# A two-layer CIN kernel: the hand-over between the layers, the place of one product in every stage, and the order of the last sums

## The chip, the core and the metric

The kernel runs on one core of a Trainium2 chip. The metric is the device time of one execution in microseconds (us). Times inside an execution are given in us from the start of the profiled span. The engines are named as the profile names them: PE (matmuls; PEld is its weight load), DVE (vector), ACT (scalar), POOL (GpSimd) and SP (issues transfers).

## The reference

Two "compressed interaction" layers work on x of 4096 rows, 32 fields and 16 embedding positions, which is 65,536 sites (row times position) of 32 values. A layer multiplies each of its channels with each field, multiplies the products with a weight matrix and normalises each output channel over all sites:

```
def _cin_layer(out, x, W, b, gamma, beta):
    h = einsum('rne,rfe->rnfe', out, x).reshape(r, -1, e)
    h = einsum('rce,oc->roe', h, W) + b[None, :, None]
    return _batchnorm(h, gamma, beta)        # over rows and positions
h1 = _cin_layer(x, x, W1, ...)               # 1024 products -> 128 channels
out, direct1 = h1[:, :64], h1[:, 64:]
direct2 = _cin_layer(out, x, W2, ...)        # 2048 products -> 128 channels
y = concatenate([direct1, direct2], axis=1).sum(axis=-1)
```

So half of layer 1 feeds layer 2, and the batch norm of layer 1 must be known before layer 2 can start: this is the boundary of the layers.

## The kernel before

**Layer 1** (lines 261 to 521) goes through 128 tiles of 512 sites. For each, DVE multiplies two loaded operands (L370), PE multiplies with W1 (L402), ACT copies the 128 result rows out of the accumulator bank (a PSUM bank, `ps`), and the 64 kept rows go to memory, to be read back in layer 2. The last four tiles (`ENDING = 4`) are handled apart: their kept halves come first, so that the statistics close early; then, still in layer 1's program, PE makes the other halves (L431), which only the direct output needs, and ACT copies these out of their banks into `ed` (the function `evict`, L515). Between the two, the scale and shift of the kept channels are computed, spread over the partitions by a tiny matmul (`keep_ps`) and copied by DVE to `keep` (L507). In the order of ACT's queue the two evictions of tile pair c = 62 come first (`queue("act", evict)`), then the first factor of layer 2; the two evictions of c = 63 are put on the list `sums_left` (it is the list `late_evictions`), from which each stage of layer 2 takes one.

**Layer 2** (L813 to L885) is one matrix product done by a fast scheme of the Strassen kind. Sites are cut into two halves and taken 512 at a time from each, so c runs from 0 to 63; the contraction is cut into four groups of fields and channels, the *stages* k = 0 to 3 of each c. I write (c,k) for a stage. In each stage:

- ACT makes two factors, `f1` and `f2` (`factor`, L647): kept rows scaled and shifted by `keep`, written to one of two PSUM buffers. It needs `keep`. It also copies a block `b11` of the products there.
- DVE makes products `zz` in two instructions (`multiply`, L637): the first, with `f1`, gives the blocks B11 and B21; the second, with `f2`, gives T3 and B22. Each block has two slices q = 0, 1 of 512 sites. The very first stage (0,0) does it in four smaller instructions, by q (`multiply_part`, L645).
- The sum T2 has two slices: POOL makes `t2[0]` (`sum_first`, L676), DVE makes `t2[1]` (L635). From these POOL makes T1 and T4 in one instruction over 2048 elements (`sum_rest`, L685; the tile is `t14`). Only at the last stage (63,3) this is in two parts, T1 and then T4.
- PE multiplies with 64 columns of weights. A product has two matmuls (q = 0, 1), and a matmul two passes in the trace; two products that write different 64-row halves run side by side, as a pair. `x2` makes X2 from B21, `x31` makes X3 (B22) and X1 (B11), `x67` makes X6 (T2) and X7 (T3), and `x54` makes X5 (T1) and X4 (T4). `x54` of a stage is not run in its own stage but in the next: the loop calls `waiting.x54()` first (L863), then `x2`, `x31` and `x67` of its own. So the products that need POOL's long instruction have a stage's time to wait for it. Stage (0,0) uses eight ordinary products and no T sums (`ordinary`).

The sums of one c lie in four banks, `x21`, `x62`, `x34` and `x57`; the pool has six banks, so c + 1 reuses those of c, and first those of layer 1. When c is done, a generator `combine` (L745) puts the seven sums together into four output blocks in `e`. Its steps are placed between the instructions of the next c's stages on ACT and DVE:

- ACT copies X1 (twice, with biases, into `both`) and X2 from `x21`.
- DVE adds `x62` to `both`; ACT makes `u2`; DVE adds `x57` to get `u3`.
- ACT copies half of `u3` into `e[low, 0]`; DVE adds `x34` to `u3`, giving `e[:, 1]` (L773: the blocks C12 and C21), and adds `x57` to `e[:, 0]` (L780: C22).
- Then the statistics: for most c, ACT sums squares about a centre (`add_square`, L569, two per c) into a column of `squares`; the centre itself comes at c = 0 from two `bn_stats` and `bn_aggr` of DVE (`first`, `moments`). The last two c use `bn_stats` of DVE (L795).
- DVE reduces `e` over the 16 positions (L800).

The **last stage** (63,3) is `at_last` (L727): after `waiting.x54()` of (63,2) it makes X6 and X1, then X2, then X5 and X7, then X3 and X4. Its `combine` has no further stage to hide under; it is followed by the closing statistics, scale and shift (L135 to L156), the scaling of the outputs (L899, L907) and their transfers.

Each engine works through its own list in order. `queue` (L226) fixes that the instructions of an engine stay in the order in which the program makes them, so the order of calls in the loop is the order of execution.

Of the kernel before, what the change touches and what calls it, by code (L numbers as in the profile page):

```python
# [43 lines left out]
ALU = mybir.AluOpType  # L44
AX = mybir.AxisListType

P = 128
# [3 lines left out]
T = 512  # L51
NC = HALF // T
# [8 lines left out]
STAGES = (3, 0, 1, 2)  # L61
# [7 lines left out]
def tile_cin(ctx: ExitStack, tc: tile.TileContext, xa, xb, xr, w1, w1m, w2, bn, out):  # L69
# [156 lines left out]
    def queue(engine, make):  # L226

        with tc.issue_after(lasts[engine].ins) if engine in lasts else nullcontext():
            lasts[engine] = make()
        return lasts[engine]  # L230
# [30 lines left out]
    with ExitStack() as one:  # L261
# [56 lines left out]

        pss = {}
        eds = {}  # L320
        late_evictions = []
        kept = {}

        def finish(t):
# [174 lines left out]
        for c in range(NC - ENDING // 2, NC):  # L499
            eds[c] = epool.tile([P, T], FP, tag="ed", name="ed")  # L500
            ks = tuple(2 * c + half - ending for half in range(2))
            if c < NC - 1:

                add_halves(banks, zs, 1, ks, False, False)
                add_leftovers_halves(banks, zr, 1, ks)
                matmul(keep_ps, spread, blocks, True, True)
                queue("dve", lambda: nc.vector.tensor_copy(keep, keep_ps))  # L507
            else:
                add_halves(banks, zs, 1, ks, True, True)
            for half, k in enumerate(ks):  # L510
                at = half_of[1 - half]
                bias = (b1, b1_swapped)[half][at]
                to = eds[c][half_of[half]]

                def evict(to=to, at=at, bias=bias, k=k):  # L515
                    return nc.scalar.activation(to, banks[k][at], AF.Identity, bias=bias)  # L516

                if c < NC - 1:
                    queue("act", evict)
                else:  # L520
                    late_evictions.append(evict)

    direct = const.tile([P, 2], FP, tag="direct", name="direct")

# [43 lines left out]
    def add_square(c, s, e):  # L568
        return nc.scalar.activation(  # L569
            unread, e[:, s], AF.Square, bias=center[:, s], accum_out=squares[:, s, c : c + 1]  # L570
        )
# [104 lines left out]
        queue("pool", lambda: nc.gpsimd.tensor_tensor(t2[:, 0], z[:, 1, 0], z[:, 0, 0], ALU.add))  # L676
        return t2

    def sum_rest(z, b11, t2, apart):

        t14 = upool.tile([P, 2, 2, T], FP, tag="t14", name="t14")
        add(t2[:, 1], z[:, 1, 1], b11)
        twice = t2.unsqueeze(1).to_broadcast([P, 2, 2, T])
        for k in (slice(0, 1), slice(1, 2)) if apart else (slice(0, 2),):
            queue("pool", lambda: nc.gpsimd.tensor_tensor(t14[:, k], z[:, 2:4][:, k], twice[:, k], ALU.subtract))  # L685
        return t2, t14

    class Stage:
# [7 lines left out]
                t2, t14 = t  # L696
                self.t2, self.t1, self.t4 = ([x[:, q] for q in range(2)] for x in (t2, t14[:, 0], t14[:, 1]))

        def one(self, x, k, b, q):
            self.sums.matmul(x, self.w[q][k], b[q], self.ends and q == 1)  # L700

        def ordinary(self):
            for q in range(2):
# [20 lines left out]
                self.one(6, 5, self.t2, q)  # L724
                self.one(7, 6, self.t3, q)

        def at_last(self):  # L727

            for q in range(2):
                self.one(6, 5, self.t2, q)  # L730
                self.one(1, 0, self.b11, q)
            self.x2()
            for q in range(2):
                self.one(5, 4, self.t1, q)
                self.one(7, 6, self.t3, q)
            for q in range(2):
                self.one(3, 7, self.b22, q)
                self.one(4, 3, self.t4, q)
# [6 lines left out]
    def combine(c, sums_):  # L745

        x21, x62, x34, x57 = sums_.banks
        both = cpool.tile([P, T], FP, tag="both", name="both")
        act(both[low], x21[high])
        act(both[high], x21[high], bias=b2_swapped[high])  # L750
        e = cpool.tile([P, 2, T], FP, tag="e", name="e")
        act(e[high, 0], x21[low])
        yield

        add(both, both, x62)
        if c == NC - 1:

            add(e[high, 0], e[high, 0], both[high])
        yield
        u2 = cpool.tile([P, T], FP, tag="u2", name="u2")  # L760
        act(u2[low], both[low], bias=b2[low])
        act(u2[high], both[low], bias=b2_swapped[low])
        yield

        u3 = cpool.tile([P, T], FP, tag="u3", name="u3")
        add(u3, u2, x57)
        yield
        act(e[low, 0], u3[high])
        if c < NC - 1:
            act(x57[high], both[high])  # L770
        yield

        add(e[:, 1], u3, x34)  # L773
        yield
        if 0 < c < MOST:
            queue("act", lambda: add_square(c, 1, e))
        yield

        rows = slice(0, P) if c < NC - 1 else low
        add(e[rows, 0], e[rows, 0], x57[rows])  # L780
        yield
        if c == 0:
            for s in range(2):
                dve(lambda: nc.vector.bn_stats(first[:, s], e[:, s]))
            dve(find_center)
            for s in range(2):
                act(center[:, s], moments[:, s, 0:1], scale=-1.0)
        if c < MOST:
            for s in range(2 if c == 0 else 1):
                queue("act", lambda: add_square(c, s, e))  # L790
        else:
            at = slice(1 + 2 * (c - MOST), 3 + 2 * (c - MOST))
            for s in range(2):
                stats = groups_of[s][:, at].rearrange("p a b -> p (a b)")
                dve(lambda: nc.vector.bn_stats(stats, e[:, s]))  # L795
                if s == 0:
                    queue("act", lambda: swap_group(at))
        yield
        dve(
            lambda: nc.vector.tensor_reduce(  # L800
                d2[:, :, c, :], e.rearrange("p s (r e) -> p s r e", e=EMB), AX.X, ALU.add
            )
        )
        if c % 16 == 15 or c == MOST - 1:
            sums_left.extend(lambda s=s: add_total(c // 16, s) for s in range(2))
        if c == MOST - 1:
            for s in range(2):
                sums_left.extend(most(s))
            sums_left.append(lambda: swap_group(slice(0, 1)))
        yield  # L810


    sums_left = late_evictions  # L813

    steps, steps_before = iter(()), iter(())
    waiting = None

    following = loaded(0)
    f1 = factor(following[0][STAGES[0]], STAGES[0], 0)
    for c in range(NC):  # L820
        raw, b, bx = following
        sums_ = Sums()

        for k, i in enumerate(STAGES):

            z = z2pool.tile([P, 4, 2, T], FP, tag="zz", name="zz")
            t = None
            if c == k == 0:

                f2 = factor(raw[i], i, 1)  # L830
                for q in range(2):
                    multiply_part(z[:, 0::3], f1, b, q)
                    multiply_part(z[:, 1:3], f2, bx, q)
            else:
                multiply(z[:, 0::3], f1, b)
                if k == 1:

                    next(steps, None)
                f2 = factor(raw[i], i, 1)
                b11 = factors.tile([P, T], FP, tag="f", name="b11")  # L840
                act(b11, z[:, 0, 1])
                if k == 1:

                    next(steps, None)
                multiply(z[:, 1:3], f2, bx)
                t2 = sum_first(z)

            next(steps_before if k == 0 else steps, None)
            if k == 3 and idle:
                dve(idle.pop(0))  # L850
            if c > 0 or k > 0:
                t = sum_rest(z, b11, t2, (c, k) == (NC - 1, 3))
            if k < 3:
                f1 = factor(raw[STAGES[k + 1]], STAGES[k + 1], 0)
            elif c + 1 < NC:
                following = loaded(c + 1)
                f1 = factor(following[0][STAGES[0]], STAGES[0], 0)

            next(steps, None)
            for _ in range(min(len(sums_left), 4 if c == NC - 1 else 1)):  # L860
                queue("act", sums_left.pop(0))
            stage = Stage(sums_, i, z, t, k == 3)
            if waiting:  # L863
                waiting.x54()
            if c == k == 0:
                stage.ordinary()
            elif (c, k) == (NC - 1, 3):
                stage.at_last()
            else:
                stage.x2()  # L870
                stage.x31()
                stage.x67()
            if c > 0 or k > 0:
                waiting = stage

            if c == 9 and k == 2:
                queue("act", direct_factors)
            if 10 <= c < 14 and k == 2:
                queue("act", lambda: scale_direct(c - 10))
            if c == 15 and k == 2:  # L880
                with tc.issue_after(loads[-1].ins):
                    write_direct()
        steps, steps_before = combine(c, sums_), steps
# [90 lines left out]
```

## Time and profile before

| what | value |
|---|---|
| median of 4 runs (lowest to highest) | 2049.69 us (2049.47 to 2050.06) |
| the profiled execution: its own time | 2050.06 us |
| its span, first to last instruction | 2048.3 us |
| PE busy | 2030.2 us, 99% |
| DVE busy | 1958.9 us |
| POOL busy | 1488.7 us, nearly all of it from 499 us on |
| ACT busy | 1186.1 us |
| layer 2's first matmul | 492.93 us |
| layer 2's last matmul begins | 2033.86 us |
| granted clock of PE | 0.998 |

The span is what the trace covers; the device time is 1.75 us longer. PE's busy share is close to the whole, but PE's matmuls overlap, so the way to see whether PE waits is the distance from one matmul to the next in the timeline, not the busy share. A "pair" in the timeline is two rows that start within some hundredths of a us, one for each half of the array; while PE is not held up, one pair of passes starts every 0.43 us.

### The profile page before, as it was taken

How to read it: one execution, taken by the hardware profiler on the slowest of the kernel's cores; microseconds unless marked ns; L12 is line 12 of the kernel's file. 1: busy time of each engine (PE TensorE's matmuls, PEld its weight loads, DVE VectorE, ACT ScalarE, POOL GpSimd, SP SyncE). 2: the span in 40 equal slices, each digit the busy share in tenths (PEclk: the TensorE clock that was granted, in tenths of full speed). 3: DMA queues.
4: the chain of work that ended last, by engine and by line, in shares of the span. 5: the costliest groups of instructions: out<-in, count | busy, mean ns of one | idle time of the engine just before them, and what ended most of it. 6: DMA issues, size and time to landing. Idle time of an engine off the chain costs nothing.

```text
span 2048.3 us, 24470 instructions
## 1 busy us (share of the span) xinstructions
PE 2030.2 (99%) x8506; PEld 719.3 (35%) x8506; DVE 1958.9 (96%) x1519; ACT 1186.1 (58%) x1912; POOL 1488.7 (73%) x518
## 2 busy tenths in 40 slices
PE   9999999999999999999999999999999999999997
PEld 3444444443333333333333333333333333333332
DVE  8998988988999999999999999999999999999997
ACT  4555555554556666565666555656656565566554
POOL 0000000002999999999999999999999999999996
PEclk9999999999999999999999999999999999999999
DMA  9999999996777776777776667777766777776661
GB/s 393 361 351 368 353 362 370 367 363 186 171 179 180 178 173 169 199 174 183 179 176 167 175 170 180 174 183 178 175 169 171 176 174 182 179 175 172 174 155 41
DMA packets 112092, 440.70 MB, mean 215 GB/s; under 512 B 13024, under 2 KB 13024, under 8 KB 103520
## 3 DMA queue, kind: packets, MB, share of 16 engines
q1 hardware_dynamic: 105552, 418.43, 73.0%
q10 hardware_dynamic: 6416, 20.72, 2.7%
q8 instruction: 66, 1.08, 0.2%
q14 instruction: 58, 0.48, 0.1%
HBM read 417.07 MB, written 22.02 MB: 214 GB/s over the span
## 4 chain that ended last, share of the span: by engine, by line
PE 97%; DVE 1%; POOL 1%; DMA 0%; ACT 0%; SPq 0%; issue 0%; DVEq 0%; POOLq 0%
PE x L671 74%; PE ps L402 21%; PE ps L363 2%; PE ps L431 1%; DMA b<-in_xb 0%; POOL t L685 0%; DVE zz L645 0%; DVE zz L640 0%; POOL t L676 0%; DVE z L370 0%; DVE d L899 0%; ACT u L632 0%; ACT ed L516 0%; DVE e L635 0%; ACT both L632 0%
## 5 line engine op out<-in xcount | busy, mean ns | idle before, releaser
L685 POOL TENSOR_TENSOR t<-zz,t 128x2048 f32<-128x2048 f32 (+1 forms) x256 | 1166.3, 4556 | 20.9 <-DVE t L635 1.1
L671 PE MATMUL x<-zz,s_sb 128*64 128x512 f32 x2048 | 922.5, 592 | 0.7 <-PE ps L431 0.7
L671 PE MATMUL x<-t,s_sb 128*64 128x512 f32 x2040 | 918.0, 592 | 1.4 <-POOL t L685 1.3
L671 PE MATMUL x<-zz,w_sb 128*64 128x512 f32 x2056 | 706.8, 592 | 0.0
L676 POOL TENSOR_TENSOR t<-zz 128x512 f32<-128x512 f32 x255 | 327.7, 1285 | 518.0 <-DVE zz L640 517.0
L640 DVE TENSOR_TENSOR zz<-f,bx 128x2048 f32<-128x2048 f32 x255 | 581.7, 2281 | 19.0 <-ACT f L632 18.9
L632 ACT ACTIVATE f<-a,keep 128x512 f32<-128x512 f32 x512 | 398.1, 778 | 342.4 <-DVE zz L640 281.8
L640 DVE TENSOR_TENSOR zz<-f,b 128x2048 f32<-128x2048 f32 x255 | 581.7, 2281 | 0.1
L671 PEld LDWEIGHTS x<-t,s_sb 128*64 128x64 f32 x2040 | 278.7, 137 | 585.3 <-issue 538.6
L671 PE MATMUL x<-t,w_sb 128*64 128x512 f32 x1020 | 479.6, 592 | 0.0
L402 PE MATMUL ps<-z,w_sb 128*128 128x512 f32 x992 | 434.3, 595 | 0.7 <-DVE z L370 0.6
L671 PEld LDWEIGHTS x<-zz,s_sb 128*64 128x64 f32 x2048 | 280.5, 137 | 294.0 <-issue 288.3
L370 DVE TENSOR_TENSOR z<-a,b 128x2048 f32<-128x2048 f32 (+1 forms) x129 | 292.9, 2273 | 50.4 <-PE ps L402 28.8
L402 PEld LDWEIGHTS ps<-z,w_sb 128*128 128x128 f32 x992 | 185.8, 190 | 247.0 <-issue 234.7
L671 PEld LDWEIGHTS x<-zz,w_sb 128*64 128x64 f32 x2056 | 215.2, 137 | 145.5 <-issue 127.0
L632 ACT ACTIVATE b<-zz 128x512 f32<-128x512 f32 x255 | 152.2, 597 | 185.8 <-DVE zz L640 185.8
L334 ACT ACTIVATE e<-ps,bn_sb 128x512 f32<-128x512 f32 x124 | 85.2, 687 | 220.4 <-PE ps L402 199.4
L635 DVE TENSOR_TENSOR t<-zz,b 128x512 f32<-128x512 f32 x255 | 172.7, 677 | 0.4
L671 PEld LDWEIGHTS x<-t,w_sb 128*64 128x64 f32 x1020 | 139.0, 137 | 0.0
L569 ACT ACTIVATE unread<-e,center 128x512 bf16<-128x512 f32 x124 | 87.6, 707 | 0.1
L340 ACT ACTIVATE ed<-ps,bn_sb 64x512 f32<-64x512 f32 x124 | 84.8, 684 | 2.3
L113 DVE BATCH_NORM_STATS2 stats<-e 128x6 f32<-128x512 f32 x124 | 85.0, 687 | 0.0
(101 smaller groups left out, 863.1 us busy)
## 6 DMA issues: line engine op xcount, KB each, us to landing
a<-h SPq DMA_DIRECT2D x256, 512.0 KB, 4.5
a<-in_xa SPq DMA_DIRECT2D x128, 512.0 KB, 7.3
b<-in_xb SPq DMA_DIRECT2D x128, 512.0 KB, 8.1
b<-in_xb SPq DMA_DIRECT2D x64, 1024.0 KB, 8.2
bx<-in_xb SPq DMA_DIRECT2D x64, 512.0 KB, 8.3
bx<-x SPq DMA_DIRECT2D x64, 512.0 KB, 10.1
h<-kept ACTq DMA_DIRECT2D x64, 256.0 KB, 5.8
r<-in_xr SPq DMA_DIRECT2D x16, 512.0 KB, 9.0
```

What stands on the lines that cost most here:

```text
L113: nc.vector.bn_stats(self.stats[:, self.at, :], h)
L334: nc.scalar.activation(e, ps, AF.Identity, bias=b1)
L340: done = nc.scalar.activation(ed[to, :], ps[KEEP:, :], AF.Identity, bias=b1[KEEP:])
L370: return nc.vector.tensor_tensor(z[:, k], a.rearrange("p (a t) -> p a t", a=2)[:, k].unsqueeze(2).to_broadcast([P, n, 2, T]), b.rearrange( ...
L402: nc.tensor.matmul(pss[t], w1_sb[:, m, :], z[:, m // 2, m % 2, :], start=(t == m == 0), stop=(t > 0 and m == 3))
L569: return nc.scalar.activation(unread, e[:, s], AF.Square, bias=center[:, s], accum_out=squares[:, s, c : c + 1])
L632: return queue("act", lambda: nc.scalar.activation(to, source, AF.Identity, **scale_bias))
L635: return dve(lambda: nc.vector.tensor_tensor(to, x, y, ALU.add))
L640: dve(lambda: nc.vector.tensor_tensor(z, a, b.rearrange("p (k q) t -> p k q t", k=2), ALU.mult))
L671: queue("pe", lambda: nc.tensor.matmul(self.of[x], w, b, start=start, stop=stop))
L676: queue("pool", lambda: nc.gpsimd.tensor_tensor(t2[:, 0], z[:, 1, 0], z[:, 0, 0], ALU.add))
L685: queue("pool", lambda: nc.gpsimd.tensor_tensor(t14[:, k], z[:, 2:4][:, k], twice[:, k], ALU.subtract))
```

## The change

There are six edits.

1. **Boundary of the layers.** Both factors of stage (0,0) are made ahead of the two evictions of c = 62 in ACT's queue; before, the evictions came first. The evictions of c = 63 stay on `sums_left`.
2. **Place of X2.** In every stage, `x2` of the stage comes in front of `waiting.x54()` of the stage ahead of it, instead of behind it.
3. **T1 and T4 by q.** For the stages up to (1,0) POOL makes `t14` in two instructions of 1024 elements each, first slice q = 0 of T1 and T4, then q = 1. The last stage keeps its own division.
4. **Last stage.** `at_last` makes X2 first, then X6 and X1 (with q = 1 ahead of q = 0), then `x54` of the stage ahead, and then X5, X7, X3, X4 as before.
5. **C22 first.** At c = 63 the sum for C22 (`e[low, 0]` plus `x57`) is made in front of the one for C12 and C21 (`u3` plus `x34`).
6. **Squares of c = 0.** The two `add_square` of c = 0 are replaced by two activations on one column each, from the variances that `moments` already holds.

```diff
@@ layer 1
-                if c < NC - 1:
-                    queue("act", evict)
-                else:
-                    late_evictions.append(evict)
+                evictions.append(evict)
@@ sum_rest
-    def sum_rest(z, b11, t2, apart):
+    def sum_rest(z, b11, t2, by_q, by_k):
...
-        for k in (slice(0, 1), slice(1, 2)) if apart else (slice(0, 2),):
-            queue("pool", lambda: nc.gpsimd.tensor_tensor(t14[:, k], z[:, 2:4][:, k], twice[:, k], ALU.subtract))
+        parts = (slice(0, 1), slice(1, 2)), (slice(0, 2),)
+        for k in parts[not by_k]:
+            for q in parts[not by_q]:
+                queue("pool", lambda: nc.gpsimd.tensor_tensor(t14[:, k, q], z[:, 2 + k.start : 2 + k.stop, q], twice[:, k, q], ALU.subtract))
@@ Stage
-    def one(self, x, k, b, q):
-        self.sums.matmul(x, self.w[q][k], b[q], self.ends and q == 1)
+    def one(self, x, k, b, q, last=1):
+        self.sums.matmul(x, self.w[q][k], b[q], self.ends and q == last)
...
-        def at_last(self):
-            for q in range(2):
-                self.one(6, 5, self.t2, q)
-                self.one(1, 0, self.b11, q)
-            self.x2()
+        def at_last(self, before):
+            self.x2()
+            for q in (1, 0):
+                self.one(6, 5, self.t2, q, 0)
+                self.one(1, 0, self.b11, q, 0)
+            before.x54()
@@ combine
+        if c == NC - 1:
+            add(e[low, 0], e[low, 0], x57[low])
         add(e[:, 1], u3, x34)
...
-        rows = slice(0, P) if c < NC - 1 else low
-        add(e[rows, 0], e[rows, 0], x57[rows])
+        if c < NC - 1:
+            add(e[:, 0], e[:, 0], x57)
...
                 act(center[:, s], moments[:, s, 0:1], scale=-1.0)
-        if c < MOST:
-            for s in range(2 if c == 0 else 1):
-                queue("act", lambda: add_square(c, s, e))
+                act(squares[:, s, 0:1], moments[:, s, 1:2], scale=float(T))
+        elif c < MOST:
+            queue("act", lambda: add_square(c, 0, e))
@@ the loop of layer 2
-    sums_left = late_evictions
+    sums_left = evictions[2:]
...
-    f1 = factor(following[0][STAGES[0]], STAGES[0], 0)
+    f1, f2 = (factor(following[0][STAGES[0]], STAGES[0], half) for half in range(2))
+    for evict in evictions[:2]:
+        queue("act", evict)
...
-                f2 = factor(raw[i], i, 1)
                 for q in range(2):
                     multiply_part(z[:, 0::3], f1, b, q)
...
-                t = sum_rest(z, b11, t2, (c, k) == (NC - 1, 3))
+                t = sum_rest(z, b11, t2, (c, k) <= (1, 0), (c, k) == (NC - 1, 3))
...
-            if waiting:
-                waiting.x54()
             if c == k == 0:
                 stage.ordinary()
             elif (c, k) == (NC - 1, 3):
-                stage.at_last()
+                stage.at_last(waiting)
             else:
                 stage.x2()
+                if waiting:
+                    waiting.x54()
                 stage.x31()
                 stage.x67()
```

On DVE, SP and POOL no instruction is added beyond POOL's four divided ones, and DVE's order differs at one place only, the last two sums. ACT's list differs at the first factors and in the two activations of c = 0; PE's differs in every stage. No transfer is added, removed or moved.

More of the change, by code (lines that the diff above doesn't have):

```diff
@@ L320, in tile_cin @@
         eds = {}
-        late_evictions = []
+        evictions = []
         kept = {}
```

## The prediction

> **What bounds the kernel.** I read the page's busy shares first, then the chain of waits, then the timeline where the chain leaves PE.
>
> ```profile
> PE 2030.2 (99%) x8506; PEld 719.3 (35%) x8506; DVE 1958.9 (96%) x1519; ACT 1186.1 (58%) x1912; POOL 1488.7 (73%) x518
> ```
>
> PE has no room, and DVE, though at 96%, is seldom what PE waits for: the chain runs through PE for 97% of the span. It leaves PE for long at two places only. The first is the boundary; this is the chain there (start, length, what):
>
> ```profile
> 488.39 0.67 ACT ed L516
> ...
> 489.77 0.68 ACT f L632
> ...
> 490.47 4.62 DVE zz L645 x4
> 495.09 4.41 DVE zz L640 x2
> ...
> 499.62 1.29 POOL t L676
> ...
> 500.97 4.55 POOL t L685
> ...
> 505.56 14.80 PE x L671 x67
> ```
>
> The evictions stand ahead of the first factor, and at 505.56 PE waits for POOL's first `t14`. The second place is the end; the timeline of PE, ACT and DVE:
>
> ```profile
> 2026.56 0.59 PE L671 MATMUL x<-t,s_sb 128*64 128x512 f32 x1
> ...
> 2031.05 0.59 ACT L632 ACTIVATE both<-x 64x512 f32<-64x512 f32 x1 [2.61 <-PE x L671]
> ...
> 2034.58 0.69 DVE L635 TENSOR_TENSOR u<-u,x 128x512 f32<-128x512 f32 x1 [0.73 <-ACT u L632]
> ...
> 2035.37 0.69 DVE L635 TENSOR_TENSOR e<-u,x 128x512 f32<-128x512 f32 x1
> 2035.97 0.67 DVE L635 TENSOR_TENSOR e<-e,x 64x512 f32<-64x512 f32 x1
> 2036.68 0.69 DVE L795 BATCH_NORM_STATS2 groups_x<-e 128x6 f32<-128x512 f32 x1
> 2037.29 0.68 DVE L795 BATCH_NORM_STATS2 groups<-e 128x6 f32<-128x512 f32 x1
> ```
>
> PE's last matmul begins at 2033.86, so it ends near 2034.45; the last sums begin only at 2035.37. The end hangs on ACT's `both` at 2031.05 and what follows from it. Between 553.95 and 2034 PE's pairs follow each other at 0.43 us: 14 pairs, 6.01 us a stage.
>
> **Edit 1, factors first.** `keep` is copied at 488.71 in 0.17 us, so `f1` can start at 488.92 (0.03 from DVE's end to ACT, as elsewhere) and takes 0.78: DVE starts at 489.72 instead of 490.47, **0.75 earlier**. Behind `f2` the two evictions end near 491.7, 1.9 later than now. They free the banks of X3 and X5, which the third product of PE needs at 492.2: covered by 0.5 us; beyond that each us would be lost in full. PE's own rows of layer 1 (L431) end at 492.25 with the next due 0.2 to 0.4 earlier, so they just don't hold up the first product, which moves from 492.93 to 492.18.
>
> **Edits 2 and 3 at the boundary.** In the kernel before, the last pair of (0,1) starts at 503.68, the next was due at 504.11 and came at 505.56: 1.45 lost. After, all of it 0.75 earlier, X2 of (0,2) takes two pairs from 503.36 (its B21 is ready at 501.87: `multiply` at 500.33, 2.29 long, less 0.75), and X5 with X4 start at 504.22 for q = 0 and at 505.08 for q = 1. POOL starts `t2` at 498.87; what halves of `t14` take, the last stage shows:
>
> ```profile
> 2021.66 4.57 POOL L685 TENSOR_TENSOR t<-zz,t 128x2048 f32<-128x2048 f32 x1
> ...
> 2027.55 4.69 POOL L685 TENSOR_TENSOR t<-zz,t 128x1024 f32<-128x1024 f32 x2
> ```
>
> The first half is ready at 498.87 + 1.35 + 2.37 = 502.6, the second at 504.92: both in time, the second by 0.16. The stall of 1.45 goes; with the 0.75 PE leads by **2.20**.
>
> [...] POOL's back-to-back period is 5.87 now (505.47 to 511.36 is 5.89) against PE's 6.01. The row gives 4.69 - 4.57 = 0.12 more per divided instruction. [...] At (1,1) the bill comes by either, since its `t14` is undivided: POOL's fifth delivery is at 498.87 + 4 x 6.00 + 1.36 + 4.58 = 528.8, PE wants it at 503.36 + 4 x 6.01 + 0.86 = 528.26. [...] I take the row: it is the same operation at nearly the same shape. [...] From here POOL gains 0.1 a stage again.
>
> **Edit 6.** At 536.24 to 537.90 ACT's two `add_square` of c = 0 (0.9 each with the accumulator's reading) stand in front of `f2` of (2,0); DVE idles 0.50 for it, POOL then 0.41 and 0.44, and PE's pair at 553.95 is 0.27 late (the last started at 553.25). Two one-column activations of about 0.2 take 1.4 less, so DVE's 0.50 goes and **0.27** with it. If ACT weren't relieved, the 0.86 more that `x54` now has to wait would cover the same 0.27.
>
> **What stops the lead.** ACT and DVE lead by only 0.75 + 0.50 = 1.25. X3 of c + 1 takes the bank of `x21` and waits for ACT's copy of X2: for c = 3 the copy (567.34) ends at 567.93, and X3 starts at 568.60: a margin of about 0.6. So PE can lead by at most about 1.85; 2.20 - 0.6 + 0.27 = 1.87 is just at this limit. I take **1.85**. From 567.74 to 664.27 PE needs 96.53 for what at 24.04 a c is 96.2: some 0.35 is lost to DVE, POOL and ACT, which have extra work for the direct output there. I leave it in; if the later `x54` covers it, 2.2.
>
> **Edit 2 in the other stages.** X2 moves forward by 1.72 (four pairs) and `x54` back by 0.86. X2's first wait is on DVE's first `multiply`, for example 2015.14 to 2017.42 against use at 2022.26: nearly 5 us of cover. `x54` gets more time for POOL, which is often last in the weight loads' waits (109 times, 40 us) without costing PE anything. Its sums are read by DVE's `u3` at 2013.95, PE being through with them at 2010.4: 3.5 us of cover, 2.7 left. On PE the count stays at 14 pairs; the rows show no price for a change of tile (2008.10 to 2008.53 is 0.43 from X6/X7 to X5/X4). Cost nothing.
>
> **Edits 4 and 5, the end.** On before's clock X2, X6, X1 run as the six pairs from 2026.56. POOL's `t2[0]` (2026.18 + 1.30) is ready at 2027.48 for its pair at 2028.28, DVE's `t2[1]` at 2026.95 for 2027.42: covered by 0.8 and 0.5. The last of these pairs starts at 2028.70 and ends at 2029.29, so ACT's `both` starts at 2029.33, 1.72 earlier; ACT is idle from 2028.44. The other pairs keep their times, T1 at 2029.9 for 2030.85 and T4 at 2032.24 for 2032.57. Then the steps with before's lengths: `both` on ACT to 2030.61, DVE's sum to 2031.34, `u2` to 2032.82, `u3` 2032.86 to 2033.54 (X5 and X7 end at 2032.72), ACT's copy into `e` to 2034.21, C22 2034.25, then C12 and C21 at 2034.85 (PE is through at 2034.45), and the two statistics at 2035.45 and 2036.06 instead of 2036.68 and 2037.29. In the old order the chain behind C22 had 0.71 between dependent instructions where independent ones have 0.60. **Gain 1.23**; everything behind is the same. From below 0.4, if ACT's copy or another small step takes longer than its neighbour's row; from above 1.6, where PE's end is the bound.
>
> **Sum.** 1.85 + 1.23 = 3.1. The profiled execution took 2050.06 (span 2048.3 and 1.75 around it), so it would take 2047.0; it was the slowest of the four, 0.37 above the median. On the median: 2049.69 - 3.1 = **2046.6**.
>
> **Rivals.**
> - *The lead is eaten.* PE can't lead by more than what feeds it, and the margins of 0.6 are smaller, or POOL's halves dearer: then PE keeps 0.75 to 1.25, or the end gives half: about 2 in all, 2047.6. For it: DVE at 96%, and POOL last in 109 loads. Against: the margins are read directly.
> - *Nothing eats it.* Halves free, no bank limit, and the 0.35 covered too: 2.20 - 0.1 + 0.27 + 0.35 + 1.23 = 3.95; 2045.7, with a larger end gain just beyond 4.1.
> - *Slower: a price in every stage.* If PE's new order of banks (X2 between X6/X7 and X5/X4) costs at the turn from one product to the next, by a weight load that isn't hidden or a bank in use, it is paid in some 251 stages: at 0.04 us it is 10 us, 2056.6. It passes the gain from 3.1 / 251 = 0.012 us a stage, and 0.2% on the slow side from 0.029. Against it: 0.14 us of load under 0.43, and no turn in the trace that costs.
> - *It doesn't do what it says:* the orders of the lists are changed as described, so no chance worth a number.
>
> **Chances.** Forecast with its own range 2046.0 to 2047.1: 0.58; lead eaten: 0.20; nothing eats it: 0.14; price in every stage: 0.08. The range 2045.5 to 2048.2 leaves out the last and a little on the low side. 0.2% is 4.1 us (about what a measurement can tell from no change): beyond it on the fast side lies half of the third case and a tail of the first, 0.13; slower 0.07; within 0.80.
>
> **What would show it.** The first layer-2 matmul near 492.2; no wait before X5 of (0,1), a wait of about 0.6 near 528.3 on POOL, none near 552; X3 of (2,0), (3,0) close behind ACT's copy; 0.43 between pairs throughout; ACT's `both` starting about 5.1 before the last matmul's end, against 3.4 now; the last statistics 1.6 after that end, against 2.8. A pitch over 6.01 a stage in the middle would make me wrong, as would a lead under 1 at 700 us.

## The result, and the profile after

The changed kernel takes 2046.47 us in the median of 41 runs (2046.02 to 2049.2), the kernel before 2049.72 in the median of 61. The ratio is 0.9986, with a 95% interval of 0.9981 to 0.999: 3.25 us less, where 2046.6 was forecast. It lies within the 0.2% that the prediction called no change, though the interval excludes 1.

The two profiled executions can't be laid over each other as they are: in the changed kernel's one, layer 1, which is the same in both, happens to be 0.64 us earlier (PE's first L431 starts at 475.17 against 475.80). So two lengths are measured inside each trace. The **length** runs from the start of DVE's copy of `keep` (L507) to the start of PE's last matmul; the **tail** from there to the start of the last `bn_stats`.

| | copy of `keep` | last matmul | length | tail |
|---|---|---|---|---|
| before | 488.71 | 2033.86 | 1545.15 | 3.43 |
| changed | 488.07 | 2031.34 | 1543.27 | 2.20 |
| gain | | | 1.88 | 1.23 |

Together that is 3.11; the spans differ by 3.8, and nearly all of the rest is the 0.64 of layer 1. The sum had said 1.85 and 1.23.

Of PE's matmuls in layer 2 the profile's list of waits has one row now (engine, line, what for, us in total, times, longest):

```profile
PE x L668 <- POOL t L684: 0.4, 1, 0.4
```

The 1.3 of before at 505.56 is gone, and so is its 0.7 ahead of layer 2's first matmul. The bill at stage (1,1), which was forecast, has come. The timeline of PE there:

```profile
526.76 1.06 PE L668 MATMUL x<-zz,w_sb 128*64 128x512 f32 x4
528.25 0.64 PE L668 MATMUL x<-t,s_sb 128*64 128x512 f32 x1 [0.43 <-POOL t L684]
```

and of POOL, whose second row is the whole `t14` of (1,1) after four divided ones:

```profile
517.62 4.71 POOL L684 TENSOR_TENSOR t<-zz,t 128x1024 f32<-128x1024 f32 x2
522.29 1.27 POOL L673 TENSOR_TENSOR t<-zz 128x512 f32<-128x512 f32 x1
523.64 4.56 POOL L684 TENSOR_TENSOR t<-zz,t 128x2048 f32<-128x2048 f32 x1
```

X2 takes the first four rows from 526.76; X5 was due at 527.62 and starts at 528.25, when POOL is done (523.64 + 4.56 = 528.20): 0.63 late. The profile's "idle 0.43" is less, since it counts from the modelled end of the matmul before. Such lateness is best read from start to start: below, a *wait* of PE is the distance of two pairs beyond 0.43.

How far PE may lead shows in the weight loads, here at (2,0) (the bracket is the idle time before a load and what ended it):

```profile
541.29 0.59 ACT L629 ACTIVATE e<-x 64x512 f32<-64x512 f32 x1
541.93 0.13 PEld L668 LDWEIGHTS x<-zz,s_sb 128*64 128x64 f32 x1 [0.60 <-ACT e L629]
...
542.97 0.68 DVE L632 TENSOR_TENSOR both<-both,x 128x512 f32<-128x512 f32 x1
...
543.70 0.13 PEld L668 LDWEIGHTS x<-zz,s_sb 128*64 128x64 f32 x1 [0.24 <-DVE both L632]
```

The load of X3 goes 0.05 after ACT's copy of X2 has ended (541.88). At X6 it is the load behind its own, that of X7, which goes 0.05 after DVE's sum has ended (543.65). From the end of these two steps to the matmuls, at 542.04 and 543.75, there are 0.16 and 0.10; before, there were 0.39 and 0.34. PE loses nothing here yet, but it has next to no more room: where PE does wait, the matmul starts 0.05 behind the step (edit 6 undone, below).

Further on it does lose. In the kernel before, four small waits of c = 3 to 7, too short for that list, were for POOL's `t14`: 0.42 in all, with the 0.05 by which the next pair is often late as well. In the changed kernel one of 0.09 is left of these, at (3,2), and X3 of (5,0), (6,0) and (7,0) waits 0.35 in all for ACT's copy of X2. The largest of each kind, first of the kernel before, then of the changed one:

```profile
626.36 0.13 PEld L671 LDWEIGHTS x<-t,s_sb 128*64 128x64 f32 x1 [0.87 <-POOL t L685]
```

```profile
614.34 0.13 PEld L668 LDWEIGHTS x<-zz,s_sb 128*64 128x64 f32 x1 [0.82 <-ACT e L629]
```

And the end, with PE's last matmul at 2031.34:

```profile
2026.82 0.59 ACT L629 ACTIVATE both<-x 64x512 f32<-64x512 f32 x1 [0.91 <-PE x L668]
...
2030.35 0.69 DVE L632 TENSOR_TENSOR u<-u,x 128x512 f32<-128x512 f32 x1
...
2031.73 0.68 DVE L632 TENSOR_TENSOR e<-e,x 64x512 f32<-64x512 f32 x1 [0.69 <-ACT e L629]
2032.34 0.67 DVE L632 TENSOR_TENSOR e<-u,x 128x512 f32<-128x512 f32 x1
2032.93 0.68 DVE L798 BATCH_NORM_STATS2 groups_x<-e 128x6 f32<-128x512 f32 x1
2033.54 0.67 DVE L798 BATCH_NORM_STATS2 groups<-e 128x6 f32<-128x512 f32 x1
```

`both` starts 4.52 ahead of the last matmul, against 2.81 before (2031.05 to 2033.86), and C22 (here the first of the two sums, at 2031.73) starts before PE's last matmul has ended (2031.34 + 0.59 = 2031.93), so before C12 and C21 could begin.

### The profile page after: what moved, and what is told of

Same layout as the page of the kernel before. It is cut to its first block, busy times and chain, and to the rows that moved or that the text cites. A ratio compares the mean times of both kernels' runs of the same rounds, so it can differ in the third digit from the quotient of the medians.

```text
span 2044.5 us, 24469 instructions
## 1 busy us (share of the span) xinstructions
PE 2029.1 (99%) x8506; PEld 861.1 (42%) x8506; DVE 1958.2 (96%) x1519; ACT 1185.0 (58%) x1910; POOL 1486.8 (73%) x522
## 4 chain that ended last, share of the span: by engine, by line
PE 98%; DVE 1%; issue 0%; DMA 0%; POOL 0%; ACT 0%; DVEq 0%; SPq 0%; POOLq 0%
PE x L668 74%; PE ps L402 21%; PE ps L363 2%; PE ps L431 1%; DMA b<-in_xb 0%; POOL t L684 0%; DVE zz L637 0%; DVE d L904 0%; ACT u L629 0%; DVE both L632 0%; ACT both L629 0%; POOL t L673 0%; DVE z L370 0%; DVE d L803 0%; DVE t L632 0%
## 5 line engine op out<-in xcount | busy, mean ns | idle before, releaser
L668 PE MATMUL x<-t,s_sb 128*64 128x512 f32 x2040 | 958.4, 592 | 0.4 <-POOL t L684 0.4
L668 PE MATMUL x<-zz,s_sb 128*64 128x512 f32 x2048 | 932.9, 592 | 0.0
L668 PE MATMUL x<-zz,w_sb 128*64 128x512 f32 x2056 | 758.4, 592 | 0.0
L668 PEld LDWEIGHTS x<-zz,w_sb 128*64 128x64 f32 x2056 | 235.3, 137 | 125.0 <-issue 122.2
```

Source lines behind the costliest of these rows:

```text
L668: queue("pe", lambda: nc.tensor.matmul(self.of[x], w, b, start=start, stop=stop))
```

## The experiments

Seven runs undo or isolate one edit each, three go further. All are judged by length and tail, from one profile each: where an edit can't touch them, lengths agree to 0.03 and tails to 0.04. The medians go with them; the kernel before, measured beside each, took 2049.38 to 2049.44.

| kernel | length | tail | median us | ratio to before, 95% interval |
|---|---|---|---|---|
| edit 1 undone | 1544.03 | 2.20 | 2047.04 | 0.9989 (0.998 to 0.9999) |
| edit 2 undone | 1543.83 | 2.23 | 2046.93 | 0.9988 (0.9978 to 0.9997) |
| edit 3 undone | 1543.28 | 2.20 | 2046.39 | 0.9987 (0.9977 to 0.9996) |
| edit 4 undone | 1543.28 | 3.86 | 2047.9 | 0.9992 (0.9983 to 1.0) |
| edit 5 undone | 1543.30 | 2.55 | 2046.65 | 0.9985 (0.9976 to 0.9994) |
| edit 6 undone | 1543.88 | 2.20 | 2047.02 | 0.9988 (0.9979 to 0.9997) |
| before, with edit 2 alone | 1544.62 | 3.39 | 2048.74 | 0.9996 (0.9987 to 1.0005) |
| direct output later | 1542.73 | 2.23 | 2045.73 | 0.9983 (0.9973 to 0.9992) |
| ... and one T2 on DVE | 1542.91 | 2.19 | 2045.88 | 0.9983 (0.9975 to 0.9992) |
| ... and X3 first instead | 1542.09 | 2.21 | 2045.26 | 0.998 (0.9971 to 0.9989) |

**Edit 1 undone.**

```diff
-    f1, f2 = (factor(following[0][STAGES[0]], STAGES[0], half) for half in range(2))
     for evict in evictions[:2]:
         queue("act", evict)
+    f1, f2 = (factor(following[0][STAGES[0]], STAGES[0], half) for half in range(2))
```

> The changed kernel with edit 1 undone: the evictions of c = 62 stand ahead of the first two factors again. Measure: from DVE's copy of keep to PE's last matmul (before 2033.86 - 488.71 = 1545.15, changed 2031.34 - 488.07 = 1543.27). Theory: everything of layer 2 starts 0.75 later and nothing gives it back, since the waits further on move along: 1544.0, time 2047.2. Rival: PE's lead is limited further on anyway (by banks that ACT and DVE free), so what is lost at the start is a stall less later: 1543.3, time 2046.5.

The length grows by 0.76, and the wait at (1,1) is 0.63, as in the changed kernel: all that feeds PE moved together, so nothing gave it back. The theory holds.

**Edit 3 undone.**

```diff
-                t = sum_rest(z, b11, t2, (c, k) <= (1, 0), (c, k) == (NC - 1, 3))
+                t = sum_rest(z, b11, t2, False, (c, k) == (NC - 1, 3))
```

> The changed kernel with edit 3 undone: POOL makes t14 whole in all stages but the last. Theory: the division only moves a loss. X5 of (0,1) waits 0.6 (due at 503.59 on the clock of the changed kernel's trace, t14 ready at 504.2), and the 0.63 at (1,1) goes, because POOL keeps its period of 5.88: 1543.3 from keep to the last matmul, time 2046.5. Rival: the division is what took the stall of 1.45 away, and the loss at (1,1) has another cause: 1543.9, time 2047.1.

Length 1543.28, the same to 0.01. The one wait on POOL is now at X5 of (0,1) (this trace is some 2.1 later than the changed kernel's):

```profile
504.86 1.06 PE L668 MATMUL x<-zz,w_sb 128*64 128x512 f32 x4
506.34 0.64 PE L668 MATMUL x<-t,s_sb 128*64 128x512 f32 x1 [0.42 <-POOL t L684]
```

Due at 505.72, it starts 0.62 late; later there is none. The division only moves the loss by four stages: it buys half an instruction's time once, and the first whole instruction gives it back.

**Edit 6 undone.**

```diff
-                act(squares[:, s, 0:1], moments[:, s, 1:2], scale=float(T))
-        elif c < MOST:
-            queue("act", lambda: add_square(c, 0, e))
+        if c < MOST:
+            for s in range(2 if c == 0 else 1):
+                queue("act", lambda: add_square(c, s, e))
```

> The changed kernel with edit 6 undone: two add_square at c = 0 again. Theory: PE's lead is limited by ACT's copy of X2 and DVE's sum of both, which free the banks of X3 and X6; both are 0.5 later, so PE waits about 0.5 at X3 and X6 of (2,0) and does not get it back: 1543.75, time 2047.0. Rival: there is no such limit, and X5 and X4, 0.86 later in their stage, cover what DVE and POOL are late: 1543.3, time 2046.5.

Length +0.61, with a new wait of 0.46 at X3 of (2,0); its row, and ACT's:

```profile
541.84 0.59 ACT L629 ACTIVATE e<-x 64x512 f32<-64x512 f32 x1
...
542.48 0.64 PE L668 MATMUL x<-zz,s_sb 128*64 128x512 f32 x1 [0.29 <-ACT e L629]
```

ACT's copy ends at 542.43 and X3 starts at 542.48. This is the limit: the bank, not POOL's sums. There is no POOL wait at (2,1), so the later X5 does cover the 0.27 of before, but that helps nothing, since the banks are late.

**Edit 2 undone**, except in the last stage.

```diff
-                stage.x2()
                 if waiting:
                     waiting.x54()
+                stage.x2()
```

> The changed kernel with edit 2 undone in all stages but the last: X5 and X4 of the stage ahead come first, then X2. Theory: X2's place is worth the 0.86 that POOL gets at the start and nothing in the other stages: a stall of 0.75 at X5's second half of (0,1), another of 0.73 at (1,1), and 0.43 between pairs everywhere else: 1544.15, time 2047.4. Rival: the division of t14 and the earlier factors alone took the stall away: 1543.3. Second rival: the place of X2 has a price in every stage, hidden by the other gains: then the middle of the trace runs faster here, by 0.01 a stage or more, 1541 or less.

The two waits are there, 0.76 and 0.70, but the length is only 0.56 more: since PE leads by less, it no longer meets the limit, and of the small waits of c = 3 to 7 (0.44 in the changed kernel) only 0.13 is left. The theory of the mechanism holds; its sum was 0.3 too high because it left out that a lead lost is also a limit not met. The second rival falls clearly: the 224 stages from (7,0) to the end of c = 62 take 1345.99 here, 1346.00 in the changed kernel and 1345.98 before, 6.009 a stage. X2's place costs and brings nothing there.

**Edit 5 undone** (C12 and C21 in front of C22), and **edit 4 undone**.

```diff
         def at_last(self, before):
-            self.x2()
-            for q in (1, 0):
-                self.one(6, 5, self.t2, q, 0)
-                self.one(1, 0, self.b11, q, 0)
             before.x54()
+            for q in range(2):
+                self.one(6, 5, self.t2, q)
+                self.one(1, 0, self.b11, q)
+            self.x2()
```

> The changed kernel with edit 5 undone: C12 and C21 summed in front of C22 at c = 63. Measure: from the start of PE's last matmul to the start of the last bn_stats (before 3.43, changed 2.20). Theory: C12 and C21 wait for PE's end, C22 queues behind them and its bn_stats must wait for it: 2.55, time 2046.8. Rival: DVE has room there, the order makes no difference: 2.20, time 2046.5.

> The changed kernel with edit 4 undone: the last stage in its old order, C22 still summed first. Theory: ACT's both comes 1.72 later, the chain behind it is late by more than PE's end, and C22 in front now makes C12 and C21 wait for ACT's copy: from the last matmul to the last bn_stats 3.9, worse than the kernel before (3.43); time 2048.2. Rival: the two edits are independent, C22 first is worth its 0.35 here too: 3.1, time 2047.4.

Tails of 2.55 and 3.86: both theories to 0.05. DVE's rows with edit 4 undone, where PE's last matmul is at 2031.32:

```profile
2031.99 0.69 DVE L632 TENSOR_TENSOR u<-u,x 128x512 f32<-128x512 f32 x1 [0.73 <-ACT u L629]
2033.37 0.68 DVE L632 TENSOR_TENSOR e<-e,x 64x512 f32<-64x512 f32 x1 [0.69 <-ACT e L629]
2033.97 0.67 DVE L632 TENSOR_TENSOR e<-u,x 128x512 f32<-128x512 f32 x1
```

C12 and C21 (third row) could have begun at 2032.7; they stand behind C22, which waits for ACT's copy. So C22 first is a gain of 0.35 when the chain is early, and a loss of 0.43 (3.86 - 3.43) when it is not.

**The kernel before with edit 2 alone.**

> The kernel before with edit 2 alone. X5 of (0,1) should wait 0.6 instead of 1.45, so PE gains 0.87 there; the 0.27 at (2,1) would be covered as well. Theory of the limit: ACT and DVE are no earlier than before, and the margins at X3 and X6 of c = 2 and 3 are 0.3 and 0.6, so PE keeps only 0.65 of it: 1544.5 from keep to the last matmul, time 2049.05. Rival, no limit: 0.87 + 0.27 + 0.35 = 1.5: 1543.65, time 2048.2.

Length 1544.62: 0.53 gained, far from 1.5. The wait at X5 of (0,1) is 0.61 instead of 1.46, so 0.85 was won there, but at X3 of (2,0) PE waits 0.51 for ACT's copy, as with edit 6 undone:

```profile
542.48 0.59 ACT L632 ACTIVATE e<-x 64x512 f32<-64x512 f32 x1
...
543.12 0.64 PE L671 MATMUL x<-zz,s_sb 128*64 128x512 f32 x1 [0.34 <-ACT e L632]
```

That settles the limit from the other side.

**Going further.** If ACT and DVE set the limit in c = 2 to 7, moving their extra work away from there should raise it. The work for the direct output, seven items of DVE with their ACT steps, was moved to c = 20 and later:

```diff
-            if k == 3 and idle:
+            if k == 3 and c >= 20 and idle:
...
-            if c == 9 and k == 2:
+            if c == 29 and k == 2:
                 queue("act", direct_factors)
```

(and likewise the scaling and the writing that follow, 20 later).

> The changed kernel with DVE's work for the direct output (seven items, one in stage 3 of each c from 0 on) moved to c = 20 and later. Theory: the limit on PE's lead in c = 2 to 7 comes from DVE's and ACT's load there; without the extra items DVE gains 0.6 per c, the small waits between 566 and 665 go, and later there is room: 1542.9 from keep to the last matmul, time 2046.1; the 0.63 at (1,1) stays, since it is POOL's. Rival: the items only take their loss along to c = 20: 1543.3.

Length 1542.73, 0.54 less than the changed kernel: all small waits are gone, and none comes up at c = 20. ACT's copy of X2 for (2,0) now ends at 540.89 instead of 541.88, so there is room again. Next, the 0.63:

> As the one with the direct work later, and in addition t14 is divided at (0,1) only, and at (0,2) DVE makes t2[0] in POOL's place. Theory: POOL gains 1.36 at once for 0.6 of DVE, so the 0.63 at (1,1) goes and PE leads up to the limit that ACT and DVE set, higher by their direct work: 1542.3, time 2045.5, better than both kernels. Rival: this sum reads two operands from SBUF while POOL works on the same block, and DVE and POOL get in each other's way for more than it saves: 1542.9 or more.

The rival won. The wait at (1,1) is gone, but one of 0.53 is there at X5 of (0,2), whose `t14` is whole in this run, and the reason that it is late is in DVE's rows:

```profile
503.37 1.36 DVE L632 TENSOR_TENSOR t<-zz 128x512 f32<-128x512 f32 x1
504.65 0.68 DVE L632 TENSOR_TENSOR t<-zz,b 128x512 f32<-128x512 f32 x1
```

The first is the new sum, the second the one DVE always makes, of the same size, with one operand in PSUM. The new one takes 1.36 instead of 0.68: POOL's `t14` ends at 504.17, and 0.56 later the new sum ends. POOL's next `t14` starts at 505.40, only 0.1 earlier than without this step (505.50 with the direct work later, where `keep` is copied at the same time).

The other way is to let PE come later for X5. For k > 0 of c = 0 and 1:

```diff
                 stage.x2()
+                if c < 2 and k > 0:
+                    stage.x31()
                 if waiting:
                     waiting.x54()
-                stage.x31()
+                if not (c < 2 and k > 0):
+                    stage.x31()
```

with `t14` divided at (0,3) only.

> As the kernel with the direct work later, and in addition, for k > 0 of c = 0 and 1, X3 and X1 come ahead of X5 and X4 of the stage before, and t14 is divided at (0,3) only. Theory: X5 then is due 2.58 behind a stage's start instead of 0.86, which is more than the 0.63 by which POOL is late; by the time the old order is back, POOL's shorter period has caught up: no stall at the boundary at all, 1542.1 from keep to the last matmul, time 2045.1. Rival: the 0.63 turns up as waits for the banks of X3 and X6 in c = 2 and later, where the lead has its limit: 1542.7, time 2045.7.

Length 1542.09, 2045.26 us: no wait is left in layer 2 but 0.1 at its first matmul, whose product DVE ends at the moment when PE would be free. Of the variants tried this is the fastest, 4.2 under the kernel before; its length is 1.18 under that of the changed kernel. What the new order gives without the other division of `t14` was not measured.

## Why the prediction was right, step by step

- **Edit 1, 0.75:** undone, it costs 0.76. PE's first matmul comes 3.48 after the copy of `keep` instead of 4.22, and 0.10 behind DVE's product in both kernels, so PE's own rows do not hold it up. The two evictions end at 491.18, 0.37 ahead of that matmul: a little less cover than the 0.5 reckoned, and what starts there is the first product, not the third.
- **Edits 2 and 3 at the boundary, lead 2.20:** no wait is left before X5 of (0,1), and stage (0,2) starts 2.20 earlier, counted from the copy of `keep`. But the prediction booked both edits together, and they are not alike: edit 3 undone costs 0.01, edit 2 undone 0.56.
- **Loss 0.6 at (1,1):** 0.63. The 0.6 in the prediction's sum is POOL's delivery at 528.8 less PE's 528.26, with 0.04 to reach PE; measured, POOL is done at 528.20 for a pair due at 527.62, and the pair starts 0.05 behind. The halves cut by q take 4.69 to 4.71 together, as the row of the last stage said (4.69), and POOL's period is 6.01 with them (498.24 to 522.29, four stages) and 5.87 to 5.89 with `t14` whole just after (522.29 to 539.92, three stages): 0.13 a stage more, where the row gave 0.12. The 0.1 that the second rival leaves for free halves is 0.6 less four times that 0.12, an estimate; no run had free halves.
- **Edit 6, 0.27:** booked in the wrong place. Undone, there is no wait on POOL at (2,1), so the later X5 covers the 0.27 without edit 6, as the prediction had noted. What the edit is worth is 0.61, and it comes through the limit, which would be that much lower without it. The prediction had put ACT's 0.50 into the limit too, so the total was not hurt.
- **The limit, 1.85:** 1.88. Counted from the copy of `keep`, the changed kernel leads the kernel before by 2.20 at (0,2), 1.57 at (1,3), 1.84 at (2,2) and 1.93 at (8,0), of which 1.88 is left at the last matmul. That the bank of X3 sets the limit was argued from margins; edit 6 undone and edit 2 alone show it, with waits of 0.46 and 0.51 released by just that copy. For the bank of X6 there is the small margin alone: no trace shows PE waiting there.
- **The 0.35 of c = 3 to 7, left in:** the size stayed, the cause did not. The later `x54` covered most of it, 0.33 of 0.42, as the other branch of the prediction had it; the limit then took 0.35 at X3. That these two are equal is luck. The move of the direct work removes them all.
- **Other stages, nothing:** 0.02 in 1346 us.
- **The end, 1.23:** 1.23, step by step: `both` 1.71 earlier against 1.72, and the end then bound by the chain through ACT's copy. One step was not foreseen: DVE's sum of `both` into `e` now runs beside POOL's `t14` and takes 1.30 instead of 0.69 (last section). It ends at 2030.24, and `u3` waits for ACT's `u2` until 2030.32 anyway. That this cost nothing is luck, by 0.08.
- **Rivals:** "the lead is eaten" is the right mechanism, but at the margins that the trace showed, not below; "nothing eats it" falls with the 0.63 and the waits at X3; "a price in every stage" is excluded by the middle.

The edits are not additive: undone one by one they cost, in length and tail, 0.76, 0.56, 0.01, 1.66, 0.35 and 0.61, which is 3.95 against 3.11 for all together.

## What to carry to other kernels

When several engines feed a busy one with little to spare, a stall removed is worth only what the next feeder allows: read each margin behind the stall, in the order of time, and let the smallest cap the gain. Dividing an instruction of an engine that keeps pace by 2% (POOL's 5.88 a stage against PE's 6.01) paid once here and cost the same when the division ended; moving its reader back, behind other work that was ready, brought no wait later. An order at the end is right only for one timing of the chains that meet there: the same swap was worth 0.35 and cost 0.43.

## What the runs showed of the hardware that was not expected

A DVE sum of two SBUF operands took about twice its time when POOL was running an instruction on SBUF as it started. With `t2[0]` on DVE it took 1.36 us for 128x512, against 0.68 for DVE's next sum of this size. The changed kernel has a clearer case, since the kernel before has the same instruction: at c = 63 DVE adds `both` to `e` (64x512, both in SBUF). The changed kernel, with POOL's `t14` running until 2029.69:

```profile
2025.00 4.69 POOL L684 TENSOR_TENSOR t<-zz,t 128x1024 f32<-128x1024 f32 x2
...
2028.93 1.30 DVE L632 TENSOR_TENSOR e<-e,both 64x512 f32<-64x512 f32 x1
```

The kernel before, where POOL has been done since 2032.24:

```profile
2033.16 0.69 DVE L635 TENSOR_TENSOR e<-e,both 64x512 f32<-64x512 f32 x1
```

With edit 4 undone the same sum starts later, at 2030.57, and takes 0.69 too.

Both long sums end shortly after POOL: 0.55 in the changed kernel (2030.24 against 2029.69), 0.56 with `t2[0]` on DVE (504.73 against 504.17). That is near the 0.60 at which DVE's instructions of this size follow each other without a wait (2031.73, 2032.34, 2032.93 and 2033.54 above). The sum with one operand in PSUM, DVE's `t2[1]`, starts with POOL running 254 times in the changed kernel's layer 2 and takes 0.67 to 0.69 each time. So in these traces a DVE sum of two SBUF operands that starts behind POOL looks as if it gets on only when POOL is done; what holds it was not shown. The other order, with DVE first, was not measured.
